# Holding the first layer's gather-fed instructions in traced order on their engines (one core, f32)

## The chip, the cores and the metric

The kernel runs on one core of a Trainium2 chip. The metric is the time of one execution on the device in microseconds (us). Engines are named as in the profile: PE is TensorE's matmul (PEld its weight load), DVE is VectorE, ACT is ScalarE, POOL is GpSimd, SP is SyncE, which only issues DMAs here.

## The reference, cut to what matters

Two layers run on 32 graphs of 512 nodes with 256 features, in f32. Only the first layer's code is touched:

```python
# graph part: u = layer norm of x, a = adjacency
h   = u @ W_msg;  msg = (a.T @ h) / max(deg, 1)
x   = x + relu(u @ W_upd + msg + bias)
# feed-forward part: v = layer norm of x, per node
t   = max over d of (v[d] + Wt[f, d]) + bt[f]          # 1024 features f
trop = s * max_p(t*sl_cvx + of_cvx) + (1-s) * min_p(t*sl_ccv + of_ccv)
y   = g * trop + (1-g) * gelu(v @ Wc + bc),  g = sigmoid(v @ Wg + bg)
x   = x + y @ Wd + bd
```

The second layer (attention over the graph, then a mixer) follows.

## The kernel before, in words

**Feed-forward part by gathers.** The maximum over 256 values of d is not computed in full. For a node whose largest entries of v stand out, only the d with v[d] above a bound can win, so the kernel takes the largest entries one after the other, gathers the row of Wt (transposed, `table`) that belongs to each, and keeps the maximum of row plus value. How many rows a node needs is counted (`counts`, column `COUNT`). The 4096 nodes of a segment (8 graphs; there are four segments) are sorted by that count into 32 tiles of 128 nodes: `put_in_order` makes the list of ranks with matmuls (L526) on one-hot matrices `lo` and `hi` and writes it as `order` (L530). Tile n takes `CAPS[n]` rows: 24, 9, 7, 6, 5, ... down to 1. A flag `over` tells afterwards whether some node had needed more (L607 compares).

**Groups.** Four tiles (g, g+8, g+16, g+24) form a group of 512 nodes; a segment has 8 groups, the program 32. The first group, (0, 7), is a light one; group (s, 0) holds its segment's tile of 24 rows. Each group passes through three generators:

- `sums`: four indirect gathers fetch the nodes' rows in sorted order (xs, L554); `ask` gathers the first row for each tile (best, L565, 512 KB, seven buffers); ScalarE normalizes (L575) and TensorE transposes (L578); a tile with more than 8 rows finds its largest entries on VectorE (L586, L587, L590); ScalarE adds the first value to best (L593); then for each further row one gather on GpSimd (L596, 512 KB, four buffers) and one combine on VectorE (L599). At the end xnT is copied (L606), the counts are compared (L607) and the bias is added to xs by a DMA (L610).
- `mixed`: for each of 8 chunks of 128 features, matmuls for gelu and gate (L623), their activations (L625), transposes of best (L630), the piecewise linear functions (L632, L636 on ScalarE, L637 accumulates on VectorE), and three VectorE operations that mix (L639 to L641).
- `down`: 64 matmuls with Wd (L652), the sum (L654), and the store to x2s (L655).

**Graph part.** `conv_in` loads x and four adjacency tiles (L390, L393), normalizes x (`layer_norm_T`, L40 to L63: statistics on VectorE, deviation on GpSimd L30 and L31, scaling on ScalarE L57, transposes L61, copies L63) and computes h (L405 to L409). `conv_out` makes the messages (L425, L435; L428, L440 on VectorE), the layer norm after them, the eight largest entries and the counts (L460 to L467), and stores the rows (L471). PSUM buffers of tag "mm" (two) are shared by the convolution, the rank lists and `down`.

**What sets the order.** `woven` draws steps from two generators in a given ratio, and each `yield` ends a step. `feed_forwards` weaves the mixing of one group with the sums of the next, and the whole is woven with `all_convs`, which computes the next segment's graph part. In this way the program is traced in one order. A scheduler then orders each engine's instructions anew: it goes by a model of how long instructions and DMAs take, and issues what the model has as ready, earlier traced work first. Each engine runs its own list strictly in the order that results. `tc.keep_in_program_order(i)` puts instruction i behind the instruction that was traced just before it on the same engine; it does not wait for anything and holds nothing else back.

Of the kernel before, what the change touches and what calls it, by code (L numbers as in the profile page):

```python
# [13 lines left out]
AF = mybir.ActivationFunctionType  # L14
ALU = mybir.AluOpType
# [6 lines left out]
D = 256  # L22
NT = N // P
# [7 lines left out]
    nc.gpsimd.tensor_tensor(rs, rs, eps[:, 1:2].to_broadcast(rs.shape), ALU.pow)  # L31


def layer_norm_T(nc, sb, ps, ident, eps, x, xnT, name, kept=None, pool=False):


    mv = sb.tile([P, NT, 2], F32, tag="ln_mv", name=f"mv{name}", bufs=2)
    for t in range(NT):
        st = sb.tile([P, 6], F32, tag="ln_st", name=f"st{name}_{t}", bufs=4)
        nc.vector.bn_stats(st, x[:, t, :])  # L40
        nc.vector.bn_aggr(mv[:, t, :], st)
    rs = sb.tile([P, NT], F32, tag="ln_rs", name=f"rs{name}", bufs=2)
    if pool:
        deviation(nc, rs, mv[:, :, 1], eps)
        shift = sb.tile([P, NT], F32, tag="ln_shift", name=f"shift{name}", bufs=2)
        nc.vector.scalar_tensor_tensor(shift, mv[:, :, 0], -1.0, rs, ALU.mult, ALU.mult)
    else:
        nc.scalar.activation(rs, mv[:, :, 1], AF.Sqrt, bias=eps[:, 0:1])
        nc.vector.reciprocal(rs, rs)
    pt = [ps.tile([P, NT, P], F32, tag="tp", name=f"lnp{name}_{c}") for c in range(DC)]  # L50
    for t in range(NT):
        if kept is None:
            xn = sb.tile([P, D], F32, tag="ln_xn", name=f"xn{name}_{t}", bufs=2 if pool else 3)
        else:
            xn = kept[:, t, :]
        if pool:
            nc.scalar.activation(xn, x[:, t, :], AF.Identity, bias=shift[:, t : t + 1], scale=rs[:, t : t + 1])  # L57
        else:
            nc.vector.tensor_scalar(xn, x[:, t, :], mv[:, t, 0:1], rs[:, t : t + 1], ALU.subtract, ALU.mult)
        for c in range(DC):  # L60
            nc.tensor.transpose(pt[c][:, t, :], xn[:, c * P : (c + 1) * P], ident)  # L61
    for c in range(DC):
        nc.scalar.copy(xnT[:, c, :], pt[c].rearrange("p t n -> p (t n)"))  # L63
# [34 lines left out]
def layer0_sorted(tc, ident, eps, x, adj, w, x2s, ranks, over, following):  # L98
# [6 lines left out]
    nc = tc.nc  # L105
    B = x.shape[0]
    SEG = B // len(x2s)
    ST = SEG * NT
# [7 lines left out]
    NG = ST // NT  # L116
# [11 lines left out]
    with ExitStack() as ctx:  # L128
# [87 lines left out]
        def features(raw):  # L216
# [167 lines left out]
                nc.gpsimd.memset(bends[:, f : f + 1], float(BENDS[f]))  # L384
            nc.vector.tensor_tensor(over[:, B * NT :], fld[:, :, NUM], bends, ALU.is_gt)

        def conv_in(b):

            xg = sa.tile([P, NT, D], F32, tag="x", name=f"x{b}")
            nc.sync.dma_start(xg, x[b].rearrange("(t p) d -> p t d", p=P))  # L390
            a = sa.tile([P, NT, N], F32R, tag="adj", name=f"adj{b}", bufs=2)
            for t in range(NT):
                nc.gpsimd.dma_start(a[:, t, :], adj[b, t * P : (t + 1) * P, :])  # L393
            x1T = sa.tile([P, DC, N], F32, tag="x1T", name=f"x1T{b}", bufs=2)
            layer_norm_T(nc, sa, ps, ident, eps, xg, x1T, f"a{b}", pool=True)
            yield

            h = sa.tile([P, NT, 2 * D + 2], F32R, tag="h", name=f"h{b}", bufs=1)
            nc.gpsimd.memset(h[:, :, D : D + 2].bitcast(F32), 1.0)
            for t0 in range(0, NT, 2):  # L400
                ph = ps.tile([P, 2, D], F32, tag="mm", name=f"ph{b}_{t0}")
                for i in range(2):
                    t = t0 + i
                    for c in range(DC):
                        nc.tensor.matmul(ph[:, i, :], x1T[:, c, t * P : (t + 1) * P], w_msg[:, c, :],  # L405
                                         start=c == 0, stop=c == DC - 1)
# [67 lines left out]
        def put_in_order(s, counts):  # L474


            n = s * ST
# [43 lines left out]
            nc.vector.tensor_mul(hi[:, 1], hi[:, 0], upto[:, :ST].unsqueeze(2).to_broadcast(shape))  # L521
            nc.vector.tensor_scalar(hi[:, 0], hi[:, 0], own_part, None, ALU.mult)
            yield
            po = ps.tile([P, N], F32, tag="mm", name=f"orderp{s}")
            for t in range(ST):
                nc.tensor.matmul(po[:, : 2 * ST], lo[:, t, :], hi[:, :, t, :], start=t == 0, stop=t == ST - 1)  # L526
            tiles = sa.tile([P, ST], F32, tag="tiles", name=f"tiles{s}", bufs=1)
            nc.vector.tensor_copy(tiles, po[:, :ST])
            nc.vector.scalar_tensor_tensor(tiles, po[:, ST : 2 * ST], float(P), tiles, ALU.mult, ALU.add)
# [4 lines left out]
        def convs(s):  # L534
            counts = sa.tile([P, ST], F32, tag="counts", name=f"counts{s}")
            yield from conv_in(s * SEG)
            for i in range(SEG):
                b = s * SEG + i
                after = conv_in(b + 1) if i + 1 < SEG else iter(())
                yield from woven(conv_out(b, counts[:, i * NT : (i + 1) * NT]), 8, after, 2)  # L540
            yield from put_in_order(s, counts)
            placed_segs.add(s)

        def feed_forwards():


            def sums(s, g):
# [14 lines left out]
                def ask(t):  # L562

                    best.append(sb.tile([P, FFN], F32, tag="best", name=f"best{s}_{g}_{t}", bufs=2 * NT - 1))
                    nc.gpsimd.indirect_dma_start(  # L565
                        out=best[t], out_offset=None, in_=table,
                        in_offset=bass.IndirectOffsetOnAxis(ap=xg[:, t, IDX : IDX + 1].bitcast(U32), axis=0))

                ask(0)
                for t, tile_no in enumerate(tiles):  # L570
                    if t + 1 < NT - 1:
                        ask(t + 1)
                    r, cap = xg[:, t, :], CAPS[tile_no]
                    xn = sb.tile([P, D], F32, tag="xn", name=f"xn{s}_{g}_{t}", bufs=2)
                    nc.scalar.activation(xn, r[:, :D], AF.Identity, bias=r[:, MEAN : MEAN + 1],  # L575
                                         scale=r[:, MEAN + 1 : MEAN + 2])
                    for c in range(DC):
                        nc.tensor.transpose(pt[c][:, t, :], xn[:, c * P : (c + 1) * P], ident)  # L578
                    vals, idxs = r[:, VAL : VAL + 8], r[:, IDX : IDX + 8]
# [10 lines left out]
                                nc.vector.match_replace(less, vals[:, eight], xn, -3e38)  # L590
                                xn = less
                    m = best[t]
                    nc.scalar.activation(m, m, AF.Identity, bias=vals[:, 0:1])  # L593
                    for k in range(1, cap):
                        row = sb.tile([P, FFN], F32, tag="rows", name=f"rows{s}_{g}_{t}_{k}", bufs=4)
                        nc.gpsimd.indirect_dma_start(  # L596
                            out=row, out_offset=None, in_=table,
                            in_offset=bass.IndirectOffsetOnAxis(ap=idxs[:, k : k + 1].bitcast(U32), axis=0))
                        nc.vector.scalar_tensor_tensor(m, row, vals[:, k : k + 1], m, ALU.add, ALU.max)  # L599
                        if k % 4 == 3:  # L600
                            yield
                    if t == NT - 2:
                        ask(NT - 1)
                    yield
                for c in range(DC):
                    nc.scalar.copy(xnT[:, c, :], pt[c].rearrange("p t n -> p (t n)"))  # L606
                nc.vector.tensor_tensor(over[:, s * ST : (s + 1) * ST].rearrange("p (t g) -> p g t", g=NG)[:, g, :],  # L607
                                        xg[:, :, COUNT], limits.rearrange("p (t g) -> p g t", g=NG)[:, g, :],
                                        ALU.is_gt)
                nc.gpsimd.dma_start(xg[:, :, :D], bd.partition_broadcast(P), accum_op=ALU.add)  # L610
                got[s, g] = xg, xnT, best

            def mixed(s, g):
# [3 lines left out]
                for f in range(FC):  # L617
# [21 lines left out]
                    nc.vector.tensor_sub(y, y, out["cls"])  # L639
                    nc.vector.scalar_tensor_tensor(y, out["gate"], 1.0, y, ALU.add, ALU.mult)  # L640
                    nc.vector.scalar_tensor_tensor(y, y, 0.5, out["cls"], ALU.mult, ALU.add)  # L641
                    yield
                got[s, g] = xg, acc

# [17 lines left out]
            for i, now in enumerate(groups):  # L662
                steps_ = mixed(*now)
                next(steps_)
                if i:
                    down(*groups[i - 1])
                yield
                more = sums(*groups[i + 1]) if i + 1 < len(groups) else iter(())
                steps = sum(1 + CAPS[n] // 4 for n in range(groups[(i + 1) % len(groups)][1], ST, NG))
                yield from woven(steps_, 9, more, steps)  # L670
            down(*groups[-1])

# [11 lines left out]
        with tc.tile_pool(name="r0", bufs=1) as raw:  # L684
            first = iter(lambda: next(ahead), 0)
            next(first)
            bounds(raw)
            for _ in woven(first, SEG * 10, features(raw), 74):
                pass
        sb = ctx.enter_context(tc.tile_pool(name="s0", bufs=2, reuse_waits="tile"))  # L690

        for _ in range(LEAD):
            next(ahead)
        for _ in woven(feed_forwards(), NG * 11 + sum(1 + cap // 4 for cap in CAPS), ahead, SEG * 12 + 5):
            pass


# [1535 lines left out]
```

## Time and profile before

| | us |
|---|---|
| median of 3 runs (4298.48 to 4301.65) | 4301.25 |
| the profiled execution, whole | 4311.61 |
| its span, first to last instruction | 4309.8 |
| PE busy | 3825.7 (89%) |
| DVE busy | 3170.3 (74%) |
| ACT busy | 2188.1 (51%) |
| POOL busy | 1584.8 (37%) |
| gathers and loads of GpSimd's queue (383 MB) | 32.0% of the DMA engines' span |
| mean granted TensorE clock | 0.949 |

The profile is of one execution. "Busy" is the time in which an engine ran instructions. A wait is idle time of an engine just before an instruction, with the one whose end released it; "issue" is idle time that nothing in the profile explains. Line numbers (L599) are those of the kernel before, also where the text speaks of the changed one; tiles are written out<-in. Periods are read from the start of the first accumulate (L637) of one group to that of the next.

### The profile page before, as it was taken

To read this page: it belongs to the slowest core of one execution; us is meant where nothing else is said; L and a number is where in the kernel's file an instruction comes from. 1 tells how busy PE (TensorE), PEld (TensorE's weight loads), DVE (VectorE), ACT (ScalarE), POOL (GpSimd) and SP (SyncE) were. 2 spreads that over 40 slices of the span, in tenths; PEclk is the share of its full clock that TensorE was granted. 3 is DMA by queue.
4 is the path that set the end of the run, shared out by engine and by line. 5 is a ranking of instruction groups with operands and counts; after the bars stand their busy time and mean duration, and the time that the engine had idled before them with its cause. 6 is when DMAs were issued, how large, how long until landed. Compare 5 with 4: busy or idle time off the path is not lost.

```text
span 4309.8 us, 56063 instructions
## 1 busy us (share of the span) xinstructions
PE 3825.7 (89%) x19799; PEld 2426.9 (56%) x19799; DVE 3170.3 (74%) x6909; ACT 2188.1 (51%) x4308; POOL 1584.8 (37%) x1973
## 2 busy tenths in 40 slices
PE   5567998989989999888999799999999999999997
PEld 4454565565655656555555355555555555555655
DVE  6668887898778987777776677767777776777763
ACT  3344655566555665555665344454444444444533
POOL 2345643565435644355331322222222223322210
PEclk8778999999999999998999899999999999999998
DMA  4547654575445754377552432333233333232210
GB/s 128 162 154 225 199 164 135 174 231 165 150 127 179 227 163 141 111 248 194 152 157 56 97 70 70 72 74 69 69 79 74 79 79 78 65 74 65 59 30 16
DMA packets 313536, 524.04 MB, mean 122 GB/s; under 512 B 104823, under 2 KB 196611, under 8 KB 313244
## 3 DMA queue, kind: packets, MB, share of 16 engines
q0 software_dynamic: 129408, 383.06, 32.0%
q1 hardware_dynamic: 183836, 137.30, 11.0%
q8 instruction: 158, 2.59, 0.2%
q14 instruction: 134, 1.10, 0.1%
HBM read 463.11 MB, written 73.95 MB: 125 GB/s over the span
## 4 chain that ended last, share of the span: by engine, by line
PE 43%; DVE 21%; DMA 10%; issue 8%; POOL 6%; ACT 4%; DVEq 0%; SPq 0%; POOLq 0%; ACTq 0%
PE clsp L623 5%; PE gatep L623 5%; PE po L652 5%; PE yTp L1341 4%; PE avp L1241 3%; DVE att L1204 3%; PE lgp L1329 3%; DVE acc L637 2%; DMA rows<-table,xs 2%; DVE best L599 2%; DMA best<-table,xs 2%; PE adp L1246 2%; DMA x<-x2s,ranks 1%; PE xp L1394 1%; PE hp L1171 1%
## 5 line engine op out<-in xcount | busy, mean ns | idle before, releaser
L623 PE MATMUL clsp<-xnT,wc 128*128 128x512 f32 x1024 | 523.4, 630 | 47.6 <-ACT cls L625 40.8
L623 PE MATMUL gatep<-xnT,wg 128*128 128x512 f32 x1024 | 496.1, 604 | 14.2 <-ACT gate L625 13.6
L652 PE MATMUL po<-wd,acc 128*128 128x256 f32 x2048 | 453.0, 380 | 4.9 <-DVE acc L641 4.0
L652 PEld LDWEIGHTS po<-wd,acc 128*128 128x128 f32 x2048 | 387.1, 190 | 72.6 <-issue 10.8
L1204 DVE SCALAR_TENSOR_TENSOR att<-own,other,mask 128x512 f32<-128x512 f32 x512 | 365.2, 741 | 57.0 <-DMA own<-ownd 56.9
L599 DVE SCALAR_TENSOR_TENSOR best<-rows,xs,best 128x1024 f32<-128x1024 f32 x212 | 271.1, 1281 | 134.3 <-ACT best L593 81.5
L637 DVE SCALAR_TENSOR_TENSOR acc<-past,fld,acc 128x512 f32<-128x512 f32 x448 | 332.6, 745 | 30.6 <-ACT past L636 22.8
L623 PEld LDWEIGHTS gatep<-xnT,wg 128*128 128x128 f32 x1024 | 195.9, 195 | 253.9 <-issue 199.9
L632 ACT ACTIVATE acc<-tz,fld 128x512 f32<-128x512 f32 x256 | 199.0, 778 | 265.5 <-PE tz L630 235.4
L596 POOL DMA_INDIRECT rows<-table,xs x212 | 258.5, 1219 | 204.3 <-DVE best L599 136.8
L636 ACT ACTIVATE past<-tz,fld 128x512 f32<-128x512 f32 x448 | 291.1, 694 | 80.1 <-DVE acc L637 79.7
L623 PEld LDWEIGHTS clsp<-xnT,wc 128*128 128x128 f32 x1024 | 184.3, 201 | 185.1 <-issue 114.7
L1241 PE MATMUL avp<-att,hv 128*32 128x512 f32 x2048 | 257.3, 605 | 30.8 <-DVE att L1204 30.8
L435 PE MATMUL pm<-h,adj 128*128 128x258 f32 (+1 forms) x1024 | 179.6, 322 | 100.5 <-DVE keep L428 39.0
L1341 PE MATMUL yTp<-sw,x 128*128 128x512 f32 x512 | 239.0, 609 | 32.0 <-DVE sw L1336 22.6
L1142 POOL DMA_INDIRECT x<-x2s,ranks x128 | 151.0, 1179 | 309.7 <-DVE x L1563 138.1
L625 ACT ACTIVATE gate<-gatep,fld 128x512 f32<-128x512 f32 x256 | 175.8, 687 | 161.6 <-PE gatep L623 132.6
L1329 PE MATMUL lgp<-wsl,x4T 128*128 128x512 f32 x512 | 244.9, 620 | 13.1 <-ACT x4T L1131 7.2
L1294 POOL TENSOR_TENSOR mu<-mu,eps 128x16 f32<-128x16 f32 x32 | 115.4, 3606 | 371.0 <-DVE mu L1293 371.0
L554 POOL DMA_INDIRECT xs<-rows_of,order x128 | 156.4, 1222 | 253.3 <-DVE acc L637 100.3
L1561 PE MATMUL outp<-v,swT 128*128 128x256 f32 x1024 | 227.4, 380 | 0.0
L435 PEld LDWEIGHTS pm<-h,adj 128*128 128x128 f32 x1024 | 150.2, 211 | 125.8 <-issue 71.3
(585 smaller groups left out, 8393.6 us busy)
## 6 DMA issues: line engine op xcount, KB each, us to landing
adj<-in_adj POOLq DMA_DIRECT2D x128, 256.0 KB
x<-added POOLq DMA_DIRECT2D x64, 512.0 KB
own<-ownd SPq DMA_DIRECT2D x128, 256.0 KB
rows_of<-keep SPq DMA_DIRECT2D x32, 550.0 KB
x<-in_x SPq DMA_DIRECT2D x32, 512.0 KB
xs<-bd POOLq DMA_DIRECT2D x32, 512.0 KB
x2s<-xs SPq DMA_DIRECT2D x32, 512.0 KB
short<-in_adj POOLq DMA_DIRECT2D x32, 512.0 KB
```

What stands on the lines that cost most here:

```text
L435: nc.tensor.matmul(pm[:, : c1 - c0], a[:, i, t * P : (t + 1) * P], h[:, i, c0:c1], start=i + c0 == 0, stop=i + 1 == NT and c0 > 0)
L596: nc.gpsimd.indirect_dma_start(out=row, out_offset=None, in_=table, in_offset=bass.IndirectOffsetOnAxis(ap=idxs[:, k : k + 1].bitcast(U32) ...
L599: nc.vector.scalar_tensor_tensor(m, row, vals[:, k : k + 1], m, ALU.add, ALU.max)
L623: nc.tensor.matmul(pf, wf[:, c, f * P : (f + 1) * P], xnT[:, c, :], start=c == 0, stop=c == DC - 1)
L636: nc.scalar.activation(r, z, AF.Relu, bias=fld[:, f, AT + b : AT + b + 1])
L637: nc.vector.scalar_tensor_tensor(y, r, fld[:, f, CH + b : CH + b + 1], y, ALU.mult, ALU.add)
L652: nc.tensor.matmul(po[:, i, :], acc[f][:, t * P : (t + 1) * P], wd[:, f, :], start=f == 0, stop=f == FC - 1)
L1204: nc.vector.scalar_tensor_tensor(e, own[h], other[:, j, h : h + 1], mask[:, j, :], ALU.max, ALU.mult)
L1241: nc.tensor.matmul(pv[p][k * HW : (k + 1) * HW, :], hv[:, j, h, e : e + HW], weighed[b, h, j], **ends)
L1329: nc.tensor.matmul(pf, xnT[:, c, t * P : (t + 1) * P], wsl[:, c, :], start=c == 0, stop=c == DC - 1)
L1341: nc.tensor.matmul(py, xn[:, t, c * P : (c + 1) * P], sw[:, t, :], start=t == 0, stop=t == NT - 1)
L1561: nc.tensor.matmul(po[:, :D], swT[:, k, t * P : (t + 1) * P], v[:, k, :], start=k == 0, stop=k == KC - 1)
```

## The change

The diff, cut to what is edited:

```diff
-def layer_norm_T(nc, sb, ps, ident, eps, x, xnT, name, kept=None, pool=False):
+def layer_norm_T(nc, sb, ps, ident, eps, x, xnT, name, kept=None, pool=False, pinned=None):
...
-        nc.vector.bn_stats(st, x[:, t, :])
+        stats = nc.vector.bn_stats(st, x[:, t, :])
+        if pinned is not None and t == 0:
+            pinned(stats)
...
+        pinned = tc.keep_in_program_order
         def conv_in(b):
...
                 nc.gpsimd.dma_start(a[:, t, :], adj[b, t * P : (t + 1) * P, :])
+            yield
             x1T = sa.tile([P, DC, N], F32, tag="x1T", name=f"x1T{b}", bufs=2)
-            layer_norm_T(nc, sa, ps, ident, eps, xg, x1T, f"a{b}", pool=True)
+            layer_norm_T(nc, sa, ps, ident, eps, xg, x1T, f"a{b}", pool=True, pinned=pinned)
...
             yield
+            yield
             po = ps.tile([P, N], F32, tag="mm", name=f"orderp{s}")
             for t in range(ST):
-                nc.tensor.matmul(po[:, : 2 * ST], lo[:, t, :], hi[:, :, t, :], start=t == 0, stop=t == ST - 1)
+                first = nc.tensor.matmul(po[:, : 2 * ST], lo[:, t, :], hi[:, :, t, :], start=t == 0, stop=t == ST - 1)
+                if t == 0:
+                    pinned(first)
...
-                yield from woven(conv_out(b, counts[:, i * NT : (i + 1) * NT]), 8, after, 2)
+                yield from woven(conv_out(b, counts[:, i * NT : (i + 1) * NT]), 8, after, 3)
...
                 ask(0)
+                yield
+                fresh = True
...
-                    nc.scalar.activation(xn, r[:, :D], AF.Identity, bias=r[:, MEAN : MEAN + 1],
-                                         scale=r[:, MEAN + 1 : MEAN + 2])
+                    normal = nc.scalar.activation(xn, r[:, :D], AF.Identity, bias=r[:, MEAN : MEAN + 1],
+                                                  scale=r[:, MEAN + 1 : MEAN + 2])
+                    if t == 0:
+                        pinned(normal)
...
-                    nc.scalar.activation(m, m, AF.Identity, bias=vals[:, 0:1])
+                    pinned(nc.scalar.activation(m, m, AF.Identity, bias=vals[:, 0:1]))
...
-                        nc.vector.scalar_tensor_tensor(m, row, vals[:, k : k + 1], m, ALU.add, ALU.max)
-                        if k % 4 == 3:
+                        larger = nc.vector.scalar_tensor_tensor(m, row, vals[:, k : k + 1], m, ALU.add, ALU.max)
+                        if fresh:
+                            pinned(larger)
+                        fresh = k % 4 == 3
+                        if fresh:
                             yield
...
                     yield
+                    fresh = True
...
-                nc.vector.tensor_tensor(over[:, s * ST : (s + 1) * ST].rearrange("p (t g) -> p g t", g=NG)[:, g, :],
-                                        xg[:, :, COUNT], limits.rearrange("p (t g) -> p g t", g=NG)[:, g, :],
-                                        ALU.is_gt)
...
+                    if f == 0:
+                        flags = over[:, s * ST : (s + 1) * ST].rearrange("p (t g) -> p g t", g=NG)
+                        pinned(nc.vector.tensor_tensor(flags[:, g, :], xg[:, :, COUNT],
+                                                       limits.rearrange("p (t g) -> p g t", g=NG)[:, g, :], ALU.is_gt))
                     yield
```

- Held in traced order: the first layer-norm statistics of each graph (VectorE), the first matmul of each segment's rank list (TensorE), the first normalization of each group and every best activation (ScalarE), and the first row combine of each step, that is, of each batch of up to four rows (VectorE).
- One more step each: between the loads of x and the adjacency and the use of x; between `hi` and the rank list's matmuls; and between a group's gathers (xs and the first best) and their use. The ratios in which `woven` draws are raised to match (`SEG * 10` to `SEG * 11`, `NG * 11` to `NG * 12`, `SEG * 12 + 5` to `SEG * 13 + 6`, `steps` by 1).
- The compare of counts (L607) moves from the end of `sums` to the first chunk of the group's own `mixed`, and is held there.

More of the change, by code (lines that the diff above doesn't have):

```diff
@@ L668, in feed_forwards @@
                 more = sums(*groups[i + 1]) if i + 1 < len(groups) else iter(())
-                steps = sum(1 + CAPS[n] // 4 for n in range(groups[(i + 1) % len(groups)][1], ST, NG))
+                steps = 1 + sum(1 + CAPS[n] // 4 for n in range(groups[(i + 1) % len(groups)][1], ST, NG))
                 yield from woven(steps_, 9, more, steps)
@@ L687, in layer0_sorted @@
             bounds(raw)
-            for _ in woven(first, SEG * 10, features(raw), 74):
+            for _ in woven(first, SEG * 11, features(raw), 74):
                 pass
@@ L693, in layer0_sorted @@
             next(ahead)
-        for _ in woven(feed_forwards(), NG * 11 + sum(1 + cap // 4 for cap in CAPS), ahead, SEG * 12 + 5):
+        for _ in woven(feed_forwards(), NG * 12 + sum(1 + cap // 4 for cap in CAPS), ahead, SEG * 13 + 6):
             pass
```

## The prediction

> **What bounds the kernel now.** I read the page's slices first.
>
> ```profile
> PE   5567998989989999888999799999999999999997
> ...
> PEclk8778999999999999998999899999999999999998
> DMA  4547654575445754377552432333233333232210
> ```
>
> Each digit is 107.7 us. Layer 0 fills slices 0 to 21 (its last down projection, L652, starts by 2357 us), and the change touches layer 0 alone. From slice 4 on TensorE is 80 to 95% busy, so TensorE is the bound, with holes. Time can be won only in those holes: from 320 to 2371 us TensorE is busy 1852.4 of 2051 us, so 199 us are idle. The second view is the waits of that stretch: who waited, for whom, us in total, times, longest.
>
> ```profile
> ACT best L593 <- DMA best<-table,xs: 119.3, 61, 6.4
> ...
> ACT past L636 <- DVE acc L637: 79.7, 35, 10.0
> ...
> DVE best L599 <- DMA rows<-table,xs: 50.5, 45, 5.2
> ...
> PE clsp L623 <- ACT cls L625: 40.8, 22, 8.4
> ...
> DVE over L607 <- DMA xs<-rows_of,order: 35.4, 12, 5.2
> ...
> PE pm L435 <- issue: 29.0, 10, 5.1
> ...
> PE pm L435 <- DVE keep L440: 23.3, 10, 5.4
> ...
> DVE sta L40 <- DMA x<-in_x: 18.3, 8, 4.4
> ...
> PE orderp L526 <- DVE hi L522: 12.1, 3, 5.4
> ...
> PE ph L405 <- ACT x1T L63: 10.7, 3, 4.3
> ```
>
> TensorE itself never waits for a gather. ScalarE and VectorE do, with ready work queued behind, and TensorE waits for that work. The timeline shows one such case (start, length, engine, in brackets the idle time and its releaser):
>
> ```profile
> 2008.76 1.15 ACT L593 ACTIVATE best<-best,xs 128x1024 f32<-128x1024 f32 x1 [6.41 <-DMA best<-table,xs]
> 2010.34 1.28 DVE L599 SCALAR_TENSOR_TENSOR best<-rows,xs,best 128x1024 f32<-128x1024 f32 x1 [4.25 <-DMA rows<-table,xs]
> ...
> 2019.35 2.64 DVE L599 SCALAR_TENSOR_TENSOR best<-rows,xs,best 128x1024 f32<-128x1024 f32 x2 [5.25 <-DMA rows<-table,xs]
> ...
> 2025.80 0.69 ACT L636 ACTIVATE past<-tz,fld 128x512 f32<-128x512 f32 x1 [9.80 <-DVE acc L637]
> ...
> 2027.12 3.78 PE L623 MATMUL clsp<-xnT,wc 128*128 128x512 f32 x4 [8.43 <-ACT cls L625]
> ```
>
> ScalarE loses 6.41 us to the best gather, VectorE 4.25 and 5.25 us to row gathers, the accumulates come late, and TensorE idles 8.43 us. Its next four matmuls take 3.78 us, where four at full clock take 1.73 (most L623 pieces of the chain of waits): a long hole costs about 2.0 us more afterwards.
>
> **The change, part by part.** Both programs hold the same instructions; only their order changes, so no engine gets more work, and layer 1's order is the same row for row.
>
> (1) *Best activations and row combines (L593, L599), and the compare (L607).* In the old order combines are bunched where one group's mixing ends and the next begins: before the first accumulate (L637) of segment 1's third group stand nine combines of the group after it; in the new order none, they alternate with accumulates from the third feature chunk on. Over the program L599 stands 21 rows later on VectorE, L593 15 later on ScalarE (L607 139 later). VectorE was busy 1618.93 us with 3088 rows from 320 to 2371 us, 0.52 us a row, so 21 rows are 11 us, against waits of at most 6.4 us: gather waits mostly go. Two gains follow. The first is TensorE's waits for L625 (40.8 + 13.6 + 6.3 us). I followed the five longest back: 8.4 and 4.1 us lead to gathers, 9.6 to the tile of 24 rows (left out, see 4), 6.5 and 5.7 to the x load. 24.7 plus a few short ones: **-28**. The second is the turnaround: the waits of L435 and L405 that VectorE's queue makes, 29.0 (named issue) + 23.3 + 7.7 + 4.2 + 3.8 = 68 us. At 1023.55 the trace has two combines (2.61 us), then L654 and L428 at 1026.08 and 1026.67, and at 1026.86 L435 after 3.08 us idle: without the combines those come 2.6 us earlier. All such holes cannot go, as accumulates now stand there; I take half, **-34** (bounds 0 and -68).
>
> (2) *Layer-norm statistics (L40) and x.* SyncE's order hardly moves (x loads stand 0 to 6 rows later, nothing else is passed), so the load is not earlier; the statistics stand 55 rows later. VectorE's 18.3 us go; on TensorE it is L405's 10.7, **-8**. What is late next is L57, 15 rows later on ScalarE, with L61 and L405 moved behind it by 40 and 11 rows; down projections cover them (64 matmuls of L652, 14.08 us in the chain at 1007 us). Uncovered it would cost back the 10.7.
>
> (3) *Ranks' matmuls (L526).* Three waits of 12.1 us and one of 5.3 before 320 us. They move 30 rows behind in segments 1 to 3; queued behind are only those same 32 matmuls (1.89 us) and the mixing. **-14** of 17.4.
>
> Sum of holes -84. About twelve of the removed ones are over 3 us, at 2.0 us of slow clock each: **-24**.
>
> [...]
>
> (4) *What is given back: the tile with 24 rows,* one in each segment. Its 23 row gathers of 512 KB feed from four buffers. In the old order its top-8 search (L586) stands 65 VectorE rows ahead of the previous mixing's first accumulate in segment 1; in the new one, 30 behind. So gathers start about 16 us after that accumulate (30 x 0.52) instead of 48 before (780 against 828). From 798.68 to 824.48 thirteen were issued, 2.15 us apart; 27 for the group are 58 us. 16 + 58, then 16 from the last combine to the group's own first accumulate (1936 to 1952), gives 90 from accumulate to accumulate; the trace has 76 (828 to 904), 75 (1366 to 1442) and 67 (1885 to 1952), so +14, +15 and +23. Against it, the fifteen combines (19 us of VectorE) that stood ahead of the first of these accumulates let it come earlier, of which (1) counts only half; I credit 6 us each. Taken: **+34**; segment 0's group already has the late form (tops at 338, accumulate at 321) and took 110 us, the upper bound for the others. Lower bound 0: VectorE has 36 us of other work in a period (111.3 busy from 766 to 904, less 30 combines of 1.28, halved), with 27 combines 71, under 76.
>
> [...]
>
> (5) *New waits.* xs gathers (L554) stand 8 rows earlier on GpSimd, best gathers (L565) 11, row gathers 6 later. What they can hold up is L30/L31 and the adjacency loads behind them; where L554 waited for the store of x2s it cost GpSimd 32.1 us in 9. And the first matmuls of a group wait for L606, 593 ns, where little stands between. I charge one L606 for each of 31 groups: **+18** (bounds 0 and 32).
>
> (6) *Start, 0 to 320 us.* The second image's statistics go from VectorE row 16 to 84, yet the first list of ranks is written at row 627 instead of 645. 0, bounds -10 and +10: latency chains fill this stretch (TensorE busy 187 of 324 us), and the sums of rows nearly cancel.
>
> **Sum:** -84 - 24 + 34 + 18 = -56, against the profiled execution: 4311.6 us (span 4309.8, 1.8 around it), so 4255.6. The median of the runs shown, 4301.25, is 10.4 lower; on its scale **4245 us**.
>
> **Rivals.**
> *A. More is won*: nothing of (4) and (5) comes true, -108: 4193. For: the stretch between two stores of group results (L655) is 59 to 60 us six times and 66.6 on average over 24. Against: gathers of 58 us cannot hide in 60.
> *B. The 24-row tiles take it back*: +26 each, halfway to the bound, -108 + 78 + 18 = -12: 4289.
> *C. Slower*: the late gathers become the bound. In segments 1 to 3 the period grows to the 110 us seen in segment 0: +34, +35 and +43, and the holes stay long, so no clock is won: -84 + 112 + 8 = +36: 4337. It decides from about +28 on each (76 + 8.6 over three). For: the one period of that shape in the trace. Against: that one lay in the start, with TensorE at 82 of 107 us for other reasons as well.
> *D. It does nothing*: excluded by the changed order.
>
> **How the numbers follow.** Forecast 0.55, A 0.17, B 0.15, C 0.13. B reaches over no change; I give 0.09 of it to faster by over 0.2% (about what a measurement of this kernel can tell) and 0.06 to within. Faster 0.81, same 0.06, slower 0.13. The range takes in A, with 8 us for the start, and B with the bounds of (5) and (6) to 4312; C is left out.
>
> **What would show it.** Right: L593's and L599's waits for DMA fall from 205 us to under 80, L607's and L526's vanish, L435's "issue" halves, TensorE's idle time from 320 to the end of layer 0 falls to about 130 us. (4) shows as the time from 24-row gathers to their group's first accumulate, and as L630 waiting for L593 or L599, which now never appears. I am wrong if layer 0 ends later than 2360 us, or if the holes return under ACT xnT L606, L57 or L30.

## The result, and the profile after

The changed kernel takes **4413.68 us** (median of 4 runs, 4408.33 to 4420.94) against 4299.86 for the kernel before (4 runs, 4297.18 to 4301.65): ratio 1.0266, 95% interval 1.0248 to 1.0285. It is slower by 114 us. The profiled execution took 4417.51 us (span 4415.4).

Where nothing else is said, the fences of this part show the changed kernel, with its own line numbers. Those used below, with the old number: L606 is L593 (first value to best), L612 L599 (combine), L637 L623, L639 L625, L650 L636, L651 L637 (accumulate), L654 L640, L670 L652 (down projection), L672 L654 (its residual add), L441 L435, L63 L61. In the text the old numbers stay.

The page's slices, each 110.4 us:

```profile
PE   4667899878998789987899689999999999999997
...
PEclk9778999999999999998999899999999999999998
DMA  5545645464552665446653423333333233332210
```

Where the kernel before had 8s and 9s from slice 4 to 20, there is now a 7 every five slices (8, 13, 18). The waits from 320 to 2480 us, about the end of layer 0 (its last down projection ends at 2462 us; engine, line, for whom; us in total, times, longest):

```profile
DVE xs L672 <- PE po L670: 245.4, 47, 7.9
POOL rows L609 <- DVE best L612: 245.3, 141, 22.7
...
ACT gate L639 <- DVE acc L654: 113.4, 24, 11.5
...
ACT best L606 <- DMA best<-table,xs: 99.3, 31, 9.1
...
DVE acc L651 <- ACT past L650: 89.4, 33, 4.6
PE clsp L637 <- ACT gate L639: 87.1, 46, 7.7
...
DVE best L612 <- DMA rows<-table,tops: 53.9, 33, 6.2
...
PE tz L644 <- ACT past L650: 17.1, 19, 2.0
...
PE lnpa L63 <- ACT xna L59: 16.5, 13, 4.1
...
PE ph L411 <- ACT x1T L65: 14.2, 7, 3.4
```

Three of these waits in the kernel before, from 320 to 2371 us:

```profile
DVE xs L654 <- PE po L652: 31.1, 7, 7.7
...
ACT gate L625 <- DVE acc L640: 24.0, 6, 11.4
...
PE clsp L623 <- ACT gate L625: 6.3, 5, 2.5
```

What the change aimed at did go: L607's 35.4 us and L526's 12.1 are no longer listed, nor L435's "issue". New at the top is VectorE standing at the residual add for TensorE's down projection, 245 us where it was 31 (235 and 21 if both are counted up to the last accumulate, as below). Behind that add stand accumulates and combines. ScalarE's gate activation waits 113 us for VectorE in the mixing (24.0 before), and TensorE waits 87 us for the gate where it had waited 6.3. All of TensorE's waits for L625 together, the term of which part (1) of the prediction took 28 off, went from 61 to 122 us.

The turnaround of one light group in the timeline of VectorE (start, length, in brackets the idle time and its releaser):

```profile
1141.29 0.42 DVE L468 FIND_INDEX8 keep<-keep,xnb 128x8 uint32<-128x256 f32 x1
1146.54 0.69 DVE L672 TENSOR_TENSOR xs<-xs,po 128x512 f32<-128x512 f32 x1 [4.83 <-PE po L670]
1151.81 2.46 DVE L651 SCALAR_TENSOR_TENSOR acc<-past,fld,acc 128x512 f32<-128x512 f32 x3 [4.58 <-ACT past L650]
```

VectorE does 0.7 us of work in 10 us. The accumulate behind the add was not ready either: it waits another 4.58 us for ScalarE. In the kernel before, the same place held combines, which waited little for their rows, and then the add without a wait:

```profile
1021.94 1.28 DVE L599 SCALAR_TENSOR_TENSOR best<-rows,xs,best 128x1024 f32<-128x1024 f32 x1 [1.51 <-DMA rows<-table,xs]
1023.55 2.61 DVE L599 SCALAR_TENSOR_TENSOR best<-rows,xs,best 128x1024 f32<-128x1024 f32 x2 [0.33 <-DMA rows<-table,xs]
1026.08 0.68 DVE L654 TENSOR_TENSOR xs<-xs,po 128x512 f32<-128x512 f32 x1
```

The two matmul groups of the mixing, after (busy us, mean ns of one, idle before them):

```profile
L637 PE MATMUL clsp<-xnT,wc 128*128 128x512 f32 x1024 | 547.7, 654 | 113.4 <-ACT gate L639 87.1 <-ACT cls L639 19.0 <-ACT xnT L623 6.5
L637 PE MATMUL gatep<-xnT,wg 128*128 128x512 f32 x1024 | 511.0, 617 | 15.6 <-ACT cls L639 10.5 <-ACT gate L639 5.1
```

Before:

```profile
L623 PE MATMUL clsp<-xnT,wc 128*128 128x512 f32 x1024 | 523.4, 630 | 47.6 <-ACT cls L625 40.8
L623 PE MATMUL gatep<-xnT,wg 128*128 128x512 f32 x1024 | 496.1, 604 | 14.2 <-ACT gate L625 13.6
```

So there are 67 us more holes here and 39 us more time in the same matmuls. Over the whole of layer 0's mixing (first accumulate of the first group to the last accumulate of all) TensorE's idle time is 2113 - 1870.5 = 242 us, against 2016 - 1826.5 = 190 before, and its busy time is 44 us longer.

**Periods** (first accumulate to first accumulate), before and after, in us:

| group | segment 0 | 1 | 2 | 3 |
|---|---|---|---|---|
| g=0, with the 24-row tile | 110, 112 | 76, 108 | 75, 108 | 67, 92 |
| g=1, with the 9-row tile | 58, 74 | 60, 77 | 59, 76 | 73, 64 |
| the others together | 340, 322 | 403, 390 | 385, 378 | 292, 292 |

(Segment 0's first group, a light one, opens the part, so five others are left there.) The first group starts 7 us later. The full periods lengthen (24-row: +93 in all, 9-row: +41) and the light ones gain only 37. One full period of each kind by engine: the stretch, its length, busy us of PE, PEld, DVE, ACT, POOL (rows), clock, DMA share, GB/s. Before, 24-row then 9-row tile:

```profile
828.00:904.00 76.00, 64.16 (x254) 43.43 (x255) 65.66 (x149) 45.01 (x82) 45.08 (x68) 0.94 0.65 201
904.00:964.00 60.00, 57.50 (x236) 38.60 (x235) 57.29 (x114) 37.74 (x65) 42.37 (x51) 0.96 0.73 226
```

After:

```profile
836.00:944.00 108.00, 84.37 (x286) 50.15 (x285) 82.35 (x169) 46.35 (x86) 57.95 (x84) 0.91 0.65 206
944.00:1021.00 77.00, 62.99 (x233) 39.87 (x233) 55.82 (x118) 39.48 (x69) 42.78 (x50) 0.91 0.58 185
```

Two different things happen. In the 24-row period VectorE has 16.7 us more work (27 combines in place of 15: twelve had been done ahead of it) and 15 us more idle time. In the 9-row period it has no more work, but idles 21 us in place of 3.

### The profile page after: what moved, and what is told of

Same layout as the page of the kernel before. It is cut to its first block, busy times and chain, and to the rows that moved or that the text cites. A ratio compares the mean times of both kernels' runs of the same rounds, so it can differ in the third digit from the quotient of the medians.

```text
span 4415.4 us, 56137 instructions
## 1 busy us (share of the span) xinstructions
PE 3872.2 (88%) x19799; PEld 2420.7 (55%) x19799; DVE 3156.3 (71%) x6909; ACT 2179.2 (49%) x4308; POOL 1595.4 (36%) x1973
## 4 chain that ended last, share of the span: by engine, by line
PE 29%; DVE 11%; DMA 4%; POOL 3%; issue 3%; ACT 2%; SPq 0%; DVEq 0%; POOLq 0%; ACTq 0%
PE yTp L1359 4%; PE avp L1259 3%; DVE att L1222 3%; PE lgp L1347 3%; PE po L670 2%; PE clsp L637 2%; PE adp L1264 2%; DMA x<-x2s,ranks 1%; PE gatep L637 1%; PE xp L1412 1%; PE hp L1189 1%; POOL x L1160 1%; DMA ownd<-turned 1%; DMA own<-ownd 1%; PE zp L1405 1%
## 5 line engine op out<-in xcount | busy, mean ns | idle before, releaser
L637 PE MATMUL clsp<-xnT,wc 128*128 128x512 f32 x1024 | 547.7, 654 | 113.4 <-ACT gate L639 87.1
L637 PE MATMUL gatep<-xnT,wg 128*128 128x512 f32 x1024 | 511.0, 617 | 15.6 <-ACT cls L639 10.5
L670 PE MATMUL po<-wd,acc 128*128 128x256 f32 x2048 | 455.6, 380 | 6.7 <-DVE acc L655 4.7
L670 PEld LDWEIGHTS po<-wd,acc 128*128 128x128 f32 x2048 | 386.4, 190 | 74.2 <-issue 9.0
L651 DVE SCALAR_TENSOR_TENSOR acc<-past,fld,acc 128x512 f32<-128x512 f32 x448 | 331.0, 744 | 98.4 <-ACT past L650 89.4
L637 PEld LDWEIGHTS clsp<-xnT,wc 128*128 128x128 f32 x1024 | 187.0, 204 | 274.1 <-issue 114.8
L637 PEld LDWEIGHTS gatep<-xnT,wg 128*128 128x128 f32 x1024 | 198.0, 200 | 245.8 <-issue 199.7
L563 POOL DMA_INDIRECT xs<-rows_of,order x128 | 169.3, 1323 | 414.1 <-DVE acc L651 203.5
L650 ACT ACTIVATE past<-tz,fld 128x512 f32<-128x512 f32 x448 | 291.1, 697 | 22.6 <-DVE acc L651 22.2
L639 ACT ACTIVATE gate<-gatep,fld 128x512 f32<-128x512 f32 x256 | 177.4, 693 | 235.2 <-PE gatep L637 119.7
L612 DVE SCALAR_TENSOR_TENSOR best<-rows,xs,best 128x1024 f32<-128x1024 f32 x212 | 270.2, 1275 | 12.0 <-DMA rows<-table,xs 12.0
L639 ACT ACTIVATE cls<-clsp,fld 128x512 f32<-128x512 f32 x256 | 177.4, 693 | 109.2 <-DVE acc L655 44.0
L672 DVE TENSOR_TENSOR xs<-xs,po 128x512 f32<-128x512 f32 x64 | 43.9, 686 | 245.4 <-PE po L670 245.4
```

The source lines that it names most:

```text
L612: larger = nc.vector.scalar_tensor_tensor(m, row, vals[:, k : k + 1], m, ALU.add, ALU.max)
L637: nc.tensor.matmul(pf, wf[:, c, f * P : (f + 1) * P], xnT[:, c, :], start=c == 0, stop=c == DC - 1)
L639: nc.scalar.activation(o, pf, fn, bias=fld[:, f, bf : bf + 1], scale=1.0 if fn == AF.Gelu else 0.5)
L650: nc.scalar.activation(r, z, AF.Relu, bias=fld[:, f, AT + b : AT + b + 1])
L651: nc.vector.scalar_tensor_tensor(y, r, fld[:, f, CH + b : CH + b + 1], y, ALU.mult, ALU.add)
L670: nc.tensor.matmul(po[:, i, :], acc[f][:, t * P : (t + 1) * P], wd[:, f, :], start=f == 0, stop=f == FC - 1)
```

## The experiments

Theories at the start: **T1**, the row gathers of the full tiles start too late, and their pace sets the period. **T2**, the holds take the combines out of the turnaround. **T3**, the held layer-norm statistics delay the graph part. Later **B**: in a full period VectorE's own work is what counts, and the change heaps it there. Times are medians; every ratio is against the kernel before on the same chip. That kernel itself took 4296 to 4308 us on the chips used, so the difference of two medians from different chips is uncertain by some 10 us; the difference of their ratios is then given as well. A step and the ratio of `woven` that is raised with it were always changed together.

### Parts of the change

**e1_xn_free**: as changed, without the hold on the first normalization and the step behind the gathers.

```diff
-                yield            # behind ask(0)
-                    if t == 0:
-                        pinned(normal)
```

> The changed kernel, but the first normalization of a group (xn, L575 of before) is not held and the step between the first gathers and their use is taken out; best activations and combines stay held. Changed kernel 4413.7 us, before 4299.9. In the order, the top-8 search of segment 1's 24-row tile moves from 30 VectorE rows behind the previous mixing's first accumulate to 36 ahead of it; no combine stands ahead of that accumulate. Theory T1 (the row gathers of the 24-row and 9-row tiles start too late, and their pace and latency then set the period): the first four gathers wait ready, the combines can start with the accumulates instead of 19 us later, so the three long periods (108, 108, 92 us) lose about 19 us each and the next ones about 10 each: near 4325, between 4300 and 4345. Theory T2 (the combines were taken out of the turnaround, where VectorE now idles 245 us for L654, and crowd the mixing): no combine returns to the turnaround of the 24-row tile, so little changes: 4390 to 4415. Theory T3 (the held layer-norm statistics, 55 rows later, delay the graph part): 4400 to 4415.

4385.95 us, 1.0177 (1.0147 to 1.0207): the row gathers of segment 1's 24-row tile start 30 us ahead of the period (813 against 843) in place of 19 behind its start, the period is 106 us in place of 108, and only 28 us come back in all (38 by the ratios). That is far from T1's 4300 to 4345 and near T2's 4390.

**e4_heavy_exempt**: in groups 0 and 1 of each segment nothing of the gathers is held.

```diff
+                held = CAPS[g] <= 8      # and every hold and the step only `if held`
```

> The changed kernel, but groups 0 and 1 of each segment (the tiles with 24 and 9 rows) hold neither xn nor best activations nor combines and have no extra step; the 24 other groups keep all. The top-8 search of the 24-row tile stands 46 rows ahead of the previous first accumulate again, 11 to 14 combines stand before it. T1: the three long periods fall back to some 75 us and the ones after them to 60 (-91 and -25), segment 0's second group by some 14, the gain of the light groups (some -39) stays: 4280, between 4265 and 4300. T2: the same direction for these groups, but the light ones still crowd their mixing, so no gain against before: 4300 to 4320. T3: above 4380, since the statistics stay held.

4393.12 us, 1.018 (1.015 to 1.021). T1 and T2 miss by 73 us and more; T3 named this number, for a reason that e14 will take away. Freed combines moved to the period ahead: that of (1,7) holds 19 combines and lasts 83 us, where the changed kernel has 5 and 69 us.

**e5_no_gather_hold** (no hold on normalization, best or combines, no step behind the gathers) and **e6_gather_hold_only** (the kernel before with just these):

> The changed kernel without any of its holds on gather-fed instructions (xn, best, combines) and without the step before xn; what is left is the graph part's step and held statistics, the rank lists' step and held matmul, and the moved and held compare. T1 and T2: the loss goes, and the waits of x, of the compare and of the rank list stay removed: 4270 to 4300. T3: the loss stays, 4380 to 4415.

> The kernel before with only the holds on xn, best and combines and the step before xn. The top-8 search of the 24-row tile stands 13 rows ahead of the previous first accumulate (in the changed kernel 30 behind), that of the 9-row tile 20 behind (17 in the changed kernel), no combine before the accumulate in any group. T1: part of the loss of the 24-row tiles stays and all of the 9-row tiles': 4340 to 4390. T2: all of the loss and more, since the compares wait as well: 4400 to 4440. T3: no loss, 4290 to 4310.

4340.48 us, 1.0068 (1.0048 to 1.0089), and 4325.76, 1.0049 (1.0031 to 1.0066). All three theories miss both numbers. Neither part alone costs near 2.66%; together they cost more than their sum. VectorE's wait at the residual add separates the two groups cleanly: 25 us in e5, 150 in e6.

**e7 to e11** take the first part apart.

```diff
 e7   before + the rank list's step and hold + the moved, held compare
 e8   before + x's step and the held statistics        e11  the step alone
 e9   as changed, without x's step and the held statistics
```

> The kernel before with only the change's edits outside the graph part and the gathers: the rank list's added step and its held first matmul, and the comparison moved behind the first block of the mixing and held. Theory T3 (of the parts that cost 0.7% together, it is the graph part's held statistics): 4290 to 4310 us, no difference from before. Theory V (it is the rank list: everything that the next segment's gathers need comes one step later): 4325 to 4350 us.

> The kernel before with only the graph part's edits: x's load one step ahead of its statistics, the first statistics of every graph held in program order, and the step counts that go with it. T3: 4325 to 4350 us, with TensorE's waits for the layer norm's normalised x (the transposes in the layer norm's helper, waiting for ScalarE) near 95 us up to the end of the last mixing, as in the four kernels run so far that hold the statistics (94 to 105), against 41 to 49 in the two that do not. V: 4295 to 4310 us.

> The changed kernel without the graph part's edits (no step ahead of the statistics, statistics not held); gathers, combines, the rank list and the comparison as changed. T3 with a sum that is simple: about the 0.5% of the gathers' holds alone, 4315 to 4335 us. Theory W (the holds of the gathers and of the graph part cost more together than apart because both fill the same stretches of VectorE): between, 4320 to 4350 us. V: 4390 to 4415 us.

> The graph part's step alone: x's load one step ahead, the step counts, and nothing held. T3 (the hold costs): 4290 to 4312 us and TensorE's waits for the normalised x back near 45 us. If the added step and not the hold costs (theory S): 4325 to 4350 us, as with the hold.

e7 4247.24 us, **0.9862** (0.9841 to 0.9883). e8 4377.76, 1.0167 (1.0145 to 1.0188). e9 4272.9, 0.9915 (0.9892 to 0.9938). e11 4322.07, 1.0032 (1.0021 to 1.0044). The change holds a gain and a loss: rank list and compare win 61 us, better than any theory said; x's edits lose 70 alone, most of it by the hold (e8 less e11: 56), and without them the changed kernel beats the kernel before. None of the ranges given for e7, e8, e9 and e11 was met. TensorE's wait for the normalised x, which T3 had named, is 90 us in e8 and 69 in e11, but 81 and 65 of these lie ahead of the first accumulate, which e8 reaches 13 us earlier than the kernel before: that wait is not where the 70 us go. The hold's price shows in the first 24-row period of e8 and e11:

```profile
308.00:445.00 137.00, 104.59 (x389) 67.11 (x389) 108.74 (x241) 69.41 (x128) 94.34 (x122) 0.89 0.75 227
```

```profile
316.00:429.00 113.00, 86.39 (x314) 51.84 (x312) 95.06 (x189) 57.68 (x101) 76.10 (x97) 0.94 0.81 249
```

With the hold, 52 more rows of VectorE fall into it, and it lasts 24 us longer.

**e12_compare_only** and **e13_rank_only** split e7's gain:

> The kernel before with one edit: the comparison with the counts stands in the mixing and is held there. Theory C (the comparison at its old place made VectorE, and all that is queued behind it, wait for the gathers of x, 35 us in the kernel before): 4250 to 4280 us. Theory R (the gain of 61 us of both edits together is the rank list's): 4290 to 4310 us.

> The kernel before with one edit: the rank list's step and its held first matmul. C: 4285 to 4305 us, the 12 to 17 us of TensorE's wait for it at most. R: 4240 to 4260 us.

4273.68 us, 0.9938 (0.9921 to 0.9955), and 4277.2, 0.995 (0.9932 to 0.9968). Both, about equal, and roughly additive (29 and 25 us of 61). C's range is met by e12; e13 falls between the two ranges, and neither theory is right about the whole.

**e14_no_stats_hold**: as changed, the statistics not held.

> The changed kernel with one thing undone: the first statistics of a graph are not held; the step ahead of them stays. T3 (the hold costs 1.4% alone and more beside the gathers' holds): 4310 to 4350 us. If what interacts is the graph part's added step: 4380 to 4410 us.

4408.85 us, 1.0252 (1.023 to 1.0274): 5 us of 114 come back. T3 falls for the changed kernel: the hold that costs 1.35% alone costs nothing here. Since e9 lacks x's step as well, it is that step, worth 0.3% alone, that costs 136 us beside the gathers' holds (145 by the ratios). In e14 the matmuls of L623 take 650 ns (99.6 us idle before them), in e9 621 (68.2).

**e15_e7_best_comb**: e7 with the holds on best and combines, but not the one on the normalization, nor the step.

> The rank list and the comparison as changed, and with them the holds on the first activation of best and on the combines, but not the hold on the normalisation and not the step behind the first gather's issue. Theory T1' (the added step, which delays the row gathers, is what the gathers' holds cost): 4235 to 4255 us, as without any hold on them. T2 (the holds take the combines out of the turnaround, whatever the step): 4265 to 4285 us, with VectorE's waits for the down projection at its residual add over 100 us.

4283.75 us, 0.9962 (0.9942 to 0.9982): T2's number, and VectorE waits 159 us at the residual add. These two holds, without the step and the first hold, give back 1.0% of e7's 1.4%; with the step and the first hold as well (e9, 0.9915) it is 0.5%.

### VectorE's work in the full period

**e17_half_combine** and **e19_e7_more_combine**:

```diff
 e17  as changed; 24-row tile: combine m[:, :FFN // 2] only
 e19  e7; 24-row tile: every second combine done twice
```

> The changed kernel, with the combines of the 24-row tile done on half of the columns only, so the other half of that tile's best is left wrong; every gather, its bytes and its place are as in the changed kernel. Theory B (VectorE's work in the long period sets its length): 23 combines at about 0.65 us in place of 1.28 take 14 us from each of the four long periods, 108 us become 92 to 98: 4355 to 4375 us. T1 (late gathers and their pace of one in 2.1 us): 27 gathers still need their 56 us, 4395 to 4415 us.

> The fastest kernel so far with every second combine of the 24-row tile done twice (the result stays the same): 12 more VectorE instructions of 1.28 us in each of the four long stretches, and not one more gather, transfer, hold or step. B: the long periods, whose VectorE was busy for 76 of 77 us, grow by what is added, 12 to 16 us each: 4290 to 4315 us. T1, or any account in which VectorE has room there: 4245 to 4260 us.

e17 4368.65 us, 1.0155 (1.0138 to 1.0172): 45 us come back with every gather as before. e19 4280.61, 0.9942 (0.9924 to 0.9959): 33 us more than e7 with nothing late, somewhat under B's range. The 24-row period of segment 1 in e17:

```profile
829.00:928.00 99.00, 80.34 (x286) 49.37 (x285) 71.07 (x169) 47.28 (x86) 56.20 (x84) 0.93 0.70 224
```

in e7:

```profile
809.00:886.00 77.00, 63.82 (x253) 43.46 (x254) 65.54 (x148) 44.73 (x81) 50.13 (x62) 0.94 0.65 197
```

and in e19:

```profile
812.00:901.00 89.00, 67.30 (x255) 44.26 (x256) 78.95 (x156) 43.45 (x78) 50.16 (x62) 0.89 0.62 190
```

11.3 us of VectorE work less shorten the period by 9, and 13.4 more lengthen it by 12: there VectorE's work passes through nearly one to one. (In segments 0 and 3 the same cut shortens the period by 18 and 25 us, more than the work taken out.) In e7 VectorE was busy for 65.5 of the 77 us, not for the 76 that e19's expectation names. In e19 nothing is late and no gather is added, so T1 is not the main cause. Its pace is in part VectorE's; the row gathers of the changed kernel from 855 to 911 us on GpSimd:

```profile
L609 POOL DMA_INDIRECT rows<-table,tops x23 | 27.2, 1181 | 15.8 <-DVE best L612 10.7 <-issue 2.6 <-DMA rows<-table,tops 1.5
```

With the four gathers of the next tiles, issuing takes 31 of the 56 us, and GpSimd waits another 11 until a combine has freed a buffer. In e17, with those combines halved, the same 27 gathers take 48 us (848 to 896); of the 8 us between, some 4 are three best gathers that stand among them in the changed kernel only.

**e18_e7_step**: e7 with the step behind the gathers, and no hold on them.

> The fastest kernel so far (rank list and comparison as changed, 4247 us) with the step behind the first gather's issue, and no hold on gathers. In its built order the long period has 13 combines and 61 rows of graph work on VectorE, where the fastest so far has 15 and 73. B: 6 us less VectorE work in two of the long periods, 4230 to 4250 us. T1 (a later start of the row gathers is what costs): 4255 to 4280 us.

4211.33 us, **0.9791** (0.9774 to 0.9808), the fastest of all and faster than both kernels. Its 24-row period:

```profile
796.00:865.00 69.00, 58.48 (x236) 39.09 (x236) 58.89 (x130) 40.83 (x71) 43.52 (x52) 0.97 0.63 196
```

6.7 us less VectorE work than e7, 8 us less time. Both ranges are missed: B has the sign, T1 has not. Counted from the start of the period, the tile's row gathers begin 4 us later than in e7 in segment 1 and 33 us later in segment 2, and these periods are 8 and 5 us shorter. The whole gain of 36 us is not the 24-row periods', though: these give 20 us over the four segments, the 9-row ones take 22 back, and the light ones give 34.

**e23_lead_17** and **e24_lead_14**: as changed, with LEAD, the number of steps that the graph part is drawn ahead of the feed-forward part, at 17 and 14 in place of 16.

> The changed kernel with the graph part one step further ahead of the feed-forward part (LEAD 17 in place of 16), every hold and step in place. In the built order the long period of segments 1 and 2 has 27 combines as before, but 54 graph rows on VectorE in place of 79, as in the kernel without the graph part's edits (52). Theory B (what falls together in the long period costs, not the holds as such): long periods of 84 to 95 us in place of 108, 4290 to 4345 us in all. If the holds and steps cost by themselves: 4395 to 4420 us.

> The changed kernel with LEAD 14: 28 combines and 90 graph rows in the long period. B: longer still, periods of 110 to 120 us, 4420 to 4450 us. If the holds and steps cost by themselves: 4395 to 4420 us.

4396.2 us, 1.0226 (1.0205 to 1.0248), and 4373.41, 1.0175 (1.0153 to 1.0196). B comes near for the period and fails for the sum; e23 meets the rival's 4395 to 4420, e24 meets neither range. In e23 the 24-row periods fall to 97 and 92 us, yet the first group starts 17 us later and light periods grow (74 for 64, 70 for 62). In e24 the long period stays at 107 to 108 and single light ones shrink to 50 and 51. Neither the full period alone nor this placing of the graph work explains the total. VectorE's wait at the residual add is still 223 and 143 us.

**What is shown and what stays open.** The wait at the residual add is 16 to 25 us in the nine kernels whose combines are free (before, e5, e7, e8, e11, e12, e13, e18, e19) and 143 to 246 in the ten where they are held in part or wholly. The holds cost 0.5% on the kernel before (e6) and 1.0% on e7 (e15). So that wait marks the holds, but it is not the loss: e9 has 157 us of it and is faster than the kernel before. The ratios of four kernels that share the rank list's and the compare's edits set the two other bundles apart:

| | without x's step and hold | with them |
|---|---|---|
| without the gathers' holds and step | 0.9862 (e7) | 1.0068 (e5) |
| with them | 0.9915 (e9) | 1.0266 (the change) |

The gathers' edits cost 0.5% alone and 2.0% beside x's; x's edits cost 2.1% alone and 3.5% beside the gathers'. The larger part of the loss is x's. In part the two meet in the 24-row period. Segment 1's in e9:

```profile
809.00:893.00 84.00, 67.41 (x246) 42.65 (x244) 72.02 (x125) 39.32 (x70) 45.30 (x57) 0.87 0.69 217
```

It has the 27 combines of the changed kernel, but 44 rows and 10 us of VectorE work less, and is 24 us shorter. Halving those combines gives 45 us back in all (e17); how much of the 114 us comes from this heap is not measured. That x's step and the gathers' holds cost far more together than apart is measured (e9 against e14, and, with x's hold, e15 against e1: 136 and 102 us, or 145 and 92 by the ratios), with TensorE's wait for the gate as its mark (20 and 84 us, 18 and 63); why the total reacts so strongly is open.

## Why the prediction was wrong

Forecast: -56 on the profiled execution; measured +106 (4417.5 against 4311.6). Of the 162 between, the 24-row periods are 57 beyond the forecast (+91 in segments 1 to 3, in place of +34), the 9-row ones +41 that it did not have, the start 7, and the light periods less segment 0's 24-row one gave 35 (37 less 2.6) where the holes and the charge of (5) had promised 84 + 24 - 18 = 90. That is 57 + 41 + 7 + 55 = 160; the rest is the end of the program. Two steps failed, (2) and (1), and (2) costs more.

- **(1) Best, combines, compare: failed.** It said "gather waits mostly go" and took the remedy to be free. The gathers' waits were to fall from 205 to under 80 us; they fell to about 165. The combines ahead of the first accumulate, which it took for the thing in the way, were useful work in a stretch where VectorE otherwise waits for L652 (31 us in the kernel before, 245 in the changed one). What was forecast at the turnaround came, and more (of the 68 us of waits that it counted 14 are left), but TensorE's waits for L625 doubled, 61 to 122 us, where 28 were to go, and those before L630 rose from 9 to 39. Measured, the gathers' edits cost 0.5% alone and 2.0% beside x's (e9 and the change against e7 and e5), where -62 us were forecast for this part. The compare, not priced by itself, is worth 29 us alone (e12).
- **(2) Statistics and x: the step that failed most.** -8 forecast, because "down projections cover" what comes later. Without x's edits the changed kernel is faster than the kernel before (e9, 0.9915); with them it is 1.0266, 141 us more (151 by the ratios). The waits that it had priced hardly moved: L405's rose from 10.7 to 14.2 us, L61's from ScalarE from 2.1 to 16.5. Alone, the hold is most of the price (e8 less e11: 56 of 70 us); next to the gathers' holds it is the step, and undoing the hold gives back nothing clear of the interval (e14). What the prediction had no term for is that (2) and (4) meet: the graph part's rows and the combines fall into the same 24-row period (VectorE 82 us in 108, in e9 72 in 84). That accounts for part of the loss; the cause of the rest stays open.
- **(3) Rank matmuls: right, and worth more.** L526's wait is gone; -14 forecast, -25 measured alone (e13).
- **Clock: wrong sign.** New holes came, and L623's matmuls take 39 us more; -24 forecast. Its 2.0 us a hole were read from one hole, of 8.43 us; that a hole costs as much from 3 us on, no run shows: before the change four matmuls of L623 took 3.78 us at a granted clock of 0.50 behind a hole of 2.46 us (at 368 us), after it 1.98 us at 1.00 behind one of 3.03 us (at 1540 us).
- **(4) The 24-row tile: mechanism half right, size wrong.** "27 for the group are 58 us" came out (56, from 855 to 911); the last gather to the last combine, 17 us more, was left out, so 19 + 56 + 17 + 16 = 108 in place of 16 + 58 + 16 = 90. But a part of the 56 us is waiting for VectorE, and what moved was the combines, not the gathers alone. The lower bound 0 argued that 71 us of VectorE work fit into 76. It halved 766 to 904 us as if they were two such periods; the 24-row period alone (828 to 904) had 65.7 us of VectorE work, 46 without its fifteen combines, so 27 combines make 81, more than the 76: the trace of before already spoke against that bound, and 82 were measured. The 9-row tile, same pattern, was not considered.
- **(5)** L623 waits for L606 three times, 6.5 us in place of the 18 charged. GpSimd's L554 waits for VectorE's accumulates, which it did not name, are at 204 us after, against 100 before.
- **(6) Start:** +7, inside its bounds.

Rival C priced the 24-row periods nearly right (+34, +35, +43; measured +33, +33, +25), but it kept all of the -84, so its 4337 is still 77 us low, and it made the late gathers the bound. e19, where VectorE's work alone lengthens the period, and e18, where a later start of the row gathers does not, speak for VectorE; its size came out right without its reason being shown. The forecast's condition for being wrong, layer 0 ending later than 2360 us, was met; the holes returned under L625, which was not on its list.

## What to carry to other kernels

Work that stands "too early" in an engine's order may be filling a wait that would otherwise stand there, as the combines did here (VectorE's wait at the residual add: 31 us before, 245 with them held): before it is held back, ask what that engine does in its place, and read the next engine's release there. Count an engine's work period by period, not over the whole: 13.4 us more of it in a period where VectorE had been busy for 65.5 of 77 us cost 12 us here (e19). And take a bundle of edits apart one by one: here two of them win 1.4% (2.1% with a third), and the bundle loses 2.7%.

## What the runs showed of the hardware

The same 1024 matmuls of L623 for gelu took 523.4 us in one order and 547.7 in the other, while the mean granted clock over the whole run moved only from 0.949 to 0.946. Holes cost again here, in the work that follows: of the 2048 matmuls of L623, 67 before and 114 after start within 3 us of the end of a TensorE hole of more than 2 us; they take 962 and 1005 ns on average, the others 605 and 613 (the two limits are chosen, not measured). In the 24-row period of the changed kernel 40 of them took 783 ns on average, 30 in the period before the change 603. From 855 to 911 us of the changed kernel 27 row gathers of 512 KB were issued, four in 1.00 and 23 in 1.18 us each on average, 31 us in all; the pace of one in 2.1 us there is that and GpSimd's waits, of which 11 us were for the combines that free the buffers.
